# Perceiver on one core: keys and values projected ahead of the first norm, key buffers filled by VectorE, slot zeros written later

## The chip, the core and the metric

The kernel runs on one core of a Trainium2 chip. A core has TensorE (PE in the profile; its weight loads are listed apart as PEld), VectorE (DVE), ScalarE (ACT), GpSimd (POOL) and SyncE (SP), and 16 DMA engines that SP, ACT and POOL can all give transfers to. The metric is the device time of one execution in microseconds (us), the median of several.

## The reference

Two layers of a perceiver: 2 batches of 256 latent rows of 256 numbers, and a context of 4096 rows of 128 numbers for each batch. Everything is float32. Each line adds a block to the residual `x`:

```python
x = x + _L0_xattn_ref(_layernorm(x), ctx_512, Wq, Wkv, Wo)     # 16 heads of 16
x = x + _L0_attn_ref(_layernorm(x), ...)                       # a state-space scan
x = x + _L0_ffn_ref(_layernorm(x), ...)                        # a spectral layer
x = x + _L1_xattn_ref(_layernorm(x), ctx_512, ctx_512, ...)
x = x + _L1_attn_ref(_layernorm(x), ...)
x = x + _L1_ffn_ref(_layernorm(x), ...)                        # 8 experts, 2 per row
```

The change lies in the first of them:

```python
Q = (x @ Wq.T).reshape(B, xN, 16, 16)
KV = (z @ Wkv.T).reshape(B, zN, 2, 16, 16)
K, V = KV[:, :, 0], KV[:, :, 1]
attn = softmax(einsum('bqhd,bkhd->bhqk', Q, K) * SCALE)
O = einsum('bhqk,bkhd->bqhd', attn, V).reshape(B, xN, DIM)
return O @ Wo.T
```

## The kernel before, in words

The first cross attention is the long part. It is cut into 8 groups (2 batches, 4 groups of 4 heads), and each group into 16 steps: 128 steps in all. `attend(n)` writes out one step. Two passes run over the scores. In the first pass (`first`, line 1020 on) a step multiplies the queries `QT[g]` with 512 keys for 4 heads, and VectorE takes the maxima of the products into `MP[G]`. When a group's 16 steps are done, its maxima are lowered into the queries (`greatest`, `lowered`). In the second pass (`second`), 17 steps behind (`LAG`), scores are formed again with keys on the partitions, ScalarE takes the exponentials, and `weigh` multiplies them with the values. So steps 0 to 16 hold the first pass only, and the two passes run side by side from step 17 on.

What a step needs is made a little ahead of it. The dictionary `made` (lines 1149 to 1170) says after which step a piece of work is written down:

- `keys(h2, c)`: one matmul over 512 context columns, two passes of TensorE's instructions, into bank `ps_k`; ScalarE copies it to a piece of `qk`.
- `place(G, c)`: four DMAs of 32 KB that put these keys into the key buffer `KB[G % 3]`, 16 rows in each quarter of the partitions, after row 0 of each quarter, which holds ones. The DMAs of group 1 are issued by ScalarE, all others by SP.
- `values_of(h2, k4)`: a group of values, that is 4 matmuls (8 instructions) over 4 x 128 context rows, into bank `ps_v`; ScalarE copies it into the tile `V`, which has 17 columns for each head: 16 of values and one of ones. The ones and a tail of zeros are written by GpSimd when the tile is new (`k4 == 0`).
- `queries(g)`: one projection (4 instructions) into `ps_q`, which ScalarE scales into `QT[g]`.
- `blank(i, c)`: fills 1024 columns of key buffer `i` with the column `one0` (a one in row 0 of each quarter, zeros elsewhere).

Ahead of step 0 lies the head. The loads of SP are `x`, `wk0`, `wq0`, two quarters of the first context `ctxT[0]`, `wv0`, and the other two quarters. Then come, as written: the norm of `x` (four tiles of 256 columns on VectorE, a square root on ScalarE), eight transposes into `ps_tr` (line 935) with two copies back (lines 937 and 939), `queries(0)`, the copy `wkc` of the key weights without their padding (line 969), the four fills of `KB[0]`, the keys of the first 512 columns for group 0 (line 1176) which go straight into `KB[0]` by ScalarE (line 1177), the work of `made[-1]` (`keys(0, 0)`, `keys(0, 1)`, `place(0, 1)`), and the fills of `KB[1]`.

The PSUM banks are split: `ps1` has four banks, shared by `ps_k`, `ps_v`, `ps_q` and the score tiles of one head (`ps_1`), and `ps2` has two tiles of two banks for the score tiles of two heads (`ps_2`). A step of the first pass takes two banks of `ps1` and one tile of `ps2`.

`route_constants` (line 297) writes small tables for the routing of the last layer, fills half of `O[1]` with zeros and writes these with 15 DMAs of GpSimd's queue to the 15 blocks of `x_slots` in DRAM, which are read at the very end. It is written down after step 50. The loads in `LATE` (steps 20 to 39) begin with a copy of a number out of `MP` into their destination, so that they wait for a step's maxima.

The order on an engine is not the order of the text alone. The program is written with a tile framework that orders each engine's instructions and adds all waits; within its model it lets a later piece go ahead where nothing holds it back. In the part from step 17 on (`in_order`), TensorE, VectorE and ScalarE keep the order of the text for what goes through `te`, `ve` and `se`.

Of the kernel before, what the change touches and what calls it, by code (L numbers as in the profile page):

```python
# [15 lines left out]
P = 128  # L16
B, NQ, D = 2, 256, 256
NT = B * NQ // P
# [32 lines left out]
def perceiver(ctx: ExitStack, tc: tile.TileContext, d: dict, out: bass.AP):  # L51
    nc = tc.nc
# [10 lines left out]
    def bank(name):  # L63
        return ps1.tile([P, 512], F32, tag="bank", name=name)
# [10 lines left out]
    def large(tag, name):  # L75
        return big.tile([P, 4096], F32, tag=tag, name=name)
# [4 lines left out]
    ident = const.tile([P, P], F32, tag="ident", name="ident")  # L81
# [5 lines left out]
    def load(name, shape, src, eng=None):  # L87
        t = const.tile(shape, F32, tag=name, name=name)
        (eng or nc.sync).dma_start(out=t, in_=src)
        return t  # L90

    def load_w(name, eng=None):
        src = d[name]
        k, n = src.shape
        return load(name, [P, k // P, n], src.rearrange("(c p) n -> p c n", p=P), eng)

    x = load("x", [P, NT, D], d["x"].rearrange("(t p) e -> p t e", p=P))
    wk0 = load_w("l0_wk")
    wq0 = load_w("l0_wq")

    one0 = const.tile([P, 1], F32, tag="one0", name="one0")
    nc.gpsimd.memset(one0, 0.0)
# [4 lines left out]
    def load_ctxT(b, c, eng):  # L107
        s = slice(c * NC // 4, (c + 1) * NC // 4)
        eng.dma_start(out=ctxT[b][:, s], in_=d["ctxT"][b, :, s])

    load_ctxT(0, 0, nc.sync)
    load_ctxT(0, 1, nc.sync)
    wv0 = load_w("l0_wv")
    load_ctxT(0, 2, nc.sync)
    load_ctxT(0, 3, nc.sync)
    cols = const.tile([P, 2, d["cols"].shape[1]], F32, tag="cols", name="cols")
# [63 lines left out]
    def rstd_of(mv):  # L180

        n = mv.shape[1]
        r = small.tile([P, n], F32, tag="rstd", name="rstd")
        ve.tensor_scalar_add(r, mv[:, :, 1], EPS)
        ve.reciprocal(r, r)
        yield
        se.activation(r, r, AF.Sqrt)
        yield
        return r
# [18 lines left out]
    def normalised(src, dst, rstd_of=rstd_of):  # L208

        n = src.shape[1]  # L210
        st = small.tile([P, n, 6], F32, tag="bnst", name="bnst")
        mv = small.tile([P, n, 2], F32, tag="bnmv", name="bnmv")
        for t in range(n):
            ve.bn_stats(st[:, t, :], src[:, t, :])
            ve.bn_aggr(mv[:, t, :], st[:, t, :])
            yield
        r = yield from rstd_of(mv)
        for t in range(n):
            ve.tensor_scalar(
                dst[:, t, :], src[:, t, :], mv[:, t, 0:1], r[:, t : t + 1], ALU.subtract, ALU.mult  # L220
            )
            yield
# [20 lines left out]
    def project(ps, w, cs, src):  # L243

        for c in range(2):
            te.matmul(ps, lhsT=w[:, c, cs], rhs=src[:, c, :], start=(c == 0), stop=(c == 1))
# [47 lines left out]
    x_slots = dram.tile([NB * P, D], F32, tag="x_slots", name="x_slots")  # L294
    y_slots = dram.tile([STORED * P, D], F32, tag="y_slots", name="y_slots")

    def route_constants(zeros):
        nc.gpsimd.memset(above, 1.0)
        nc.gpsimd.affine_select(
            out=above, in_=above, pattern=[[1, P]], compare_op=ALU.is_gt, fill=0.0, base=0, channel_multiplier=-1  # L300
        )
        nc.gpsimd.memset(ones, 1.0)
        for t, step, base in ((first_slot, P, 0), (rank, -1, E), (further, 1, 0)):
            nc.gpsimd.iota(
                t, pattern=[[step, t.shape[1]]], base=base, channel_multiplier=0, allow_small_or_imprecise_dtypes=True
            )
        nc.gpsimd.memset(zeros, 0.0)
        for k in range(NB):
            nc.gpsimd.dma_start(out=x_slots[k * P : (k + 1) * P, :], in_=zeros)
# [614 lines left out]
        yield from add_rows(b, o_all, a1_wo, bank)  # L924


    head = large("P", "head")
    xn = head[:, : NT * D].rearrange("p (t e) -> p t e", t=NT)
    xnT = head[:, NT * D : 2 * NT * D].rearrange("p (c n) -> p c n", c=2)
    for _ in normalised(x, xn):  # L930
        pass
    for c in range(2):
        ps = bank("ps_tr")
        for t in range(NT):
            nc.tensor.transpose(ps[:, t * P : (t + 1) * P], xn[:, t, c * P : (c + 1) * P], ident)
        if c:
            nc.scalar.copy(xnT[:, c, :], ps)
        else:
            nc.vector.tensor_copy(xnT[:, c, :], ps)
    O = [acts.tile([P, 2, D], F32, tag=f"O{b}", name=f"O{b}") for b in range(B)]  # L940
    layer0 = ExitStack()
    one = layer0.enter_context(pool("l0x", 1))
# [4 lines left out]
    def queries(g):  # L947
        ps = bank("ps_q")
        project(ps, wq0, slice(g * P, (g + 1) * P), xnT)
        nc.scalar.mul(QT[g], ps, DH**-0.5)  # L950

    queries(0)

# [6 lines left out]
    STEPS = NK // 2  # L962
    LAG = STEPS + 1
    HW = 8 * VW
    VT, MP, AV = {}, {}, {}
# [9 lines left out]
    KB = [large(f"K{i}", f"KB{i}") for i in range(3)]  # L975

    def blank(i, c):

        nc.scalar.copy(KB[i][:, c * 1024 : (c + 1) * 1024], one0.to_broadcast([P, 1024]))

    KC = {}

# [20 lines left out]
    def values_of(h2, k4):  # L1003

        b, half = divmod(h2, 2)
        if k4 == 0:
            vt = big.tile([P, NK * HW + 16], F32, tag=f"V{half}", name="V")
            nc.gpsimd.memset(vt[:, NK * HW :], 0.0)
            nc.gpsimd.memset(vt[:, : NK * HW].rearrange("p (k r) -> p k r", r=VW)[:, :, DH], 1.0)
            VT[h2] = vt  # L1010
        ps = bank("ps_v")
        for c in range(4):
            k = (4 * k4 + c) * P
            te.matmul(
                ps[:, c * P : (c + 1) * P],
                lhsT=ctxT[b][:, k : k + P],
                rhs=wv0[:, 0, half * P : (half + 1) * P],
                start=True,
                stop=True,
            )  # L1020
        se.copy(
            VT[h2][:, 4 * k4 * HW : 4 * (k4 + 1) * HW].rearrange("p (k r) -> p k r", r=VW)[:, :, :DH],
            ps.rearrange("p (k r) -> p k r", r=DH),
        )
# [121 lines left out]
        NM - 14 + i for i, k in enumerate((2, 2, 2, 2, 2, 2, 2, 2, 2, 1, 1, 3)) for _ in range(k)  # L1146
    ]
    chunks = NC // 512
    made = {}
    for h2 in range(B * 2):  # L1150
        for c in range(chunks):
            n0 = max(2 * c - 3, -1) if h2 == 0 else 2 * STEPS * h2 - 19 + 4 * c
            made.setdefault(n0, []).append((keys, h2, c))
            made.setdefault(n0, []).append((place, 2 * h2, c))
            n1 = max(n0, 2 * STEPS * h2 - 12 + 2 * c) if h2 else n0 + 3
            made.setdefault(n1, []).append((place, 2 * h2 + 1, c))
        for k4 in range(NK // 4):
            n0 = 2 * k4 + h2 if h2 < 2 else STEPS * (2 * h2 - 1) + 4 * k4 + 1
            made.setdefault(n0, []).append((values_of, h2, k4))
    for g in range(1, NG):  # L1160
        made.setdefault(4 * g - 1, []).append((queries, g))
    for c in range(4):
        made.setdefault(c, []).append((blank, 2, c))
    for i, f in enumerate(LATE):
        made.setdefault(20 + i, []).append((lambda f=f, i=i: f(MP[(20 + i) // STEPS][:, 0, 0, :1]),))
    made.setdefault(50, []).append((lambda: route_constants(O[1][:, 0, :]),))
    made.setdefault(NM - 10, []).append((spectral_loads,))

    ahead = state_prologue(0, lambda name: bank(name))
    for n in AHEAD:  # L1170
        made.setdefault(n, []).append((next, ahead, None))

    for c in range(4):
        blank(0, c)
    ps = bank("ps_k")
    nc.tensor.matmul(ps, lhsT=wk0[:, 0, :P], rhs=ctxT[0][:, :512], start=True, stop=True)
    nc.scalar.activation(KB[0][:, :512], ps, AF.Identity, bias=one0)
    made[-1].remove((place, 0, 0))
    for f, *at in made[-1]:
        f(*at)  # L1180
    for c in range(4):
        blank(1, c)
    behind = {}

    def attend(n):
# [127 lines left out]
    with pool("ffn", 1) as one:  # L1313
# [38 lines left out]
        ps = bank("ps_n")  # L1352
# [341 lines left out]
```

## Time and profile before

| what | us |
|---|---|
| median of 3 runs (lowest, highest) | 855.04 (854.05, 857.52) |
| the profiled execution, its own time | 854.43 |
| span of its records | 852.7 |
| busy: PE, DVE, ACT, POOL | 806.0, 581.4, 452.5, 46.3 |
| first PE instruction; first score matmul of step 0 | 8.02; 15.87 |
| first score matmul of step 4; of step 16 | 29.23; 62.93 |

The page of the profile gives busy time by engine, 40 slices of the span, and groups of instructions. The timeline lists instructions in order of time; a row has start, length (from the first start to the last end, if several are merged), engine, line, operation, tile written, tile read, how many, and in square brackets how long the engine stood idle before it and for whom. Most helpers are recorded under line 172, so a row is told by its tiles: `ps<-KB,qk` is a score matmul of the first pass, `ps_v` a group of values, `ps_k` keys, `ps_q` queries.

### The profile page before, as it was taken

The numbers are of one execution on the slowest core, as the hardware profiler recorded it, in microseconds if no ns is written. First come the engines' busy times: TensorE is split into PE (matmuls) and PEld (weight loads), VectorE is DVE, ScalarE is ACT, GpSimd is POOL, SyncE is SP. The second block draws the span as 40 slices with busy tenths as digits, with TensorE's granted clock in tenths as the row PEclk, the third lists the DMA queues.
The fourth block names the chain that finished last, engine by engine and source line by source line (L and its number), as shares of the span: only waits on it lengthen the run. The fifth ranks groups of instructions, "written<-read, shape, count | busy, mean of one in ns | idle before, by whom it ended". The sixth has DMA issues, their size and how long they took to land.

```text
span 852.7 us, 21009 instructions
## 1 busy us (share of the span) xinstructions
PE 806.0 (95%) x8626; PEld 576.9 (68%) x8626; DVE 581.4 (68%) x1076; ACT 452.5 (53%) x858; POOL 46.3 (5%) x108
## 2 busy tenths in 40 slices
PE   5998999999999999999988999989799999899996
PEld 3675666666666666666655666865568875799985
DVE  4686888887878787688797766888774588441112
ACT  6434666666667666566664788554534335311110
POOL 5004011000000000000000000000000000030003
PEclk9997999999999999999999999999999999799999
DMA  7215114001101010100000100230205411439602
GB/s 269 55 36 180 26 37 126 17 20 23 24 17 24 11 31 18 23 14 15 2 2 2 50 2 27 75 99 1 99 1 198 165 33 56 144 106 330 207 13 82
DMA packets 35315, 56.67 MB, mean 66 GB/s; under 512 B 5873, under 2 KB 22817, under 8 KB 35217
## 3 DMA queue, kind: packets, MB, share of 16 engines
q1 hardware_dynamic: 27904, 41.44, 16.0%
q0 software_dynamic: 3264, 10.05, 3.5%
q10 hardware_dynamic: 4048, 3.80, 1.6%
q8 instruction: 70, 1.15, 0.5%
q14 instruction: 29, 0.23, 0.1%
HBM read 42.16 MB, written 4.85 MB: 55 GB/s over the span
## 4 chain that ended last, share of the span: by engine, by line
PE 84%; DVE 9%; ACT 4%; issue 2%; DMA 0%; ACTq 0%; DVEq 0%
PE ps L172 29%; PE av L172 17%; PE ps_h L1474 5%; PE ps_y L1490 5%; PE ps_k L172 4%; PE ps_v L172 3%; PE ps_s L172 3%; DVE mp L172 3%; DVE states L172 2%; PE ps_aqk L172 2%; PE ps_in L172 2%; PE ps_pt L172 1%; PE ps_f L172 1%; PE ps_ht L172 1%; PE ps_am L172 1%
## 5 line engine op out<-in xcount | busy, mean ns | idle before, releaser
L172 DVE TENSOR_REDUCE mp<-ps 128x2 f32<-128x1024 f32 (+1 forms) x273 | 303.2, 1154 | 97.8 <-PE ps L172 97.7
L172 ACT ACTIVATE exps<-ps 128x512 f32<-128x512 f32 x512 | 267.1, 603 | 132.3 <-PE ps L172 132.0
L172 PE MATMUL ps<-qk,KB 32*128 32x256 f32 x2048 | 261.8, 398 | 3.4 <-ACT exps L172 1.7
L172 PE MATMUL ps<-KB,qk 32*128 32x256 f32 x2048 | 252.6, 396 | 4.5 <-DVE mp L172 4.5
L172 PEld LDWEIGHTS ps<-KB,qk 32*128 32x128 f32 x2048 | 173.8, 187 | 60.7 <-issue 34.4
L172 PEld LDWEIGHTS ps<-qk,KB 32*128 32x128 f32 x2048 | 188.6, 187 | 18.4 <-ACT exps L172 5.2
L172 PE MATMUL av<-exps,V 128*32 128x256 f32 x2048 | 137.3, 386 | 1.2 <-ACT exps L172 0.8
L172 PEld LDWEIGHTS av<-exps,V 128*32 128x32 f32 x2048 | 53.8, 109 | 63.5 <-ACT exps L172 33.3
L172 DVE TENSOR_TENSOR av<-av 128x256 f32<-128x256 f32 x120 | 49.7, 414 | 5.9 <-PE av L172 5.5
L1481 ACT ACTIVATE room<-ps_h 128x512 f32<-128x512 f32 x24 | 14.2, 598 | 72.3 <-PE ps_h L1474 55.8
L1474 PEld LDWEIGHTS ps_h<-room,w 128*128 128x128 f32 x384 | 44.5, 192 | 0.5
L1474 PE MATMUL ps_h<-room,w 128*128 128x128 f32 x384 | 44.7, 275 | 0.0
L1490 PE MATMUL ps_y<-w,room 128*128 128x256 f32 x192 | 43.3, 379 | 0.0
L172 PEld LDWEIGHTS ps_v<-l_wv,ctxT 128*128 128x128 f32 x256 | 32.6, 191 | 15.2 <-issue 6.2
L172 DVE TENSOR_TENSOR_SCAN states<-decay,ps_in 128x256 f32<-128x256 f32 x64 | 40.0, 670 | 2.5 <-PE ps_in L172 2.5
L1490 PEld LDWEIGHTS ps_y<-w,room 128*128 128x128 f32 x192 | 35.6, 190 | 4.4
L172 PE MATMUL ps_k<-ctxT,wkc 128*128 128x512 f32 x64 | 36.5, 655 | 0.0
L172 PE MATMUL av<-more,nat 128*128 128x256 f32 x128 | 33.4, 384 | 3.0 <-DVE more L172 2.9
L172 PE MATMUL ps_v<-l_wv,ctxT 128*128 128x128 f32 x256 | 35.0, 280 | 1.0 <-ACT V L172 1.0
L172 ACT COPY qk<-ps_k 128x512 f32<-128x512 f32 x32 | 18.7, 588 | 26.8 <-PE ps_k L172 26.5
L172 ACT COPY V<-ps_v 128x512 f32<-128x512 f32 x32 | 18.8, 587 | 20.8 <-PE ps_v L172 15.7
L172 PE MATMUL ps_s<-ctxT,xn 128*128 128x512 f32 x64 | 29.5, 594 | 0.0
(308 smaller groups left out, 862.9 us busy)
## 6 DMA issues: line engine op xcount, KB each, us to landing
w<-in_moe_w SPq DMA_DIRECT2D x24, 1024.0 KB, 7.6
KB<-qk SPq DMA_DIRECT2D x220, 32.0 KB, 2.0
ctxT<-in_ctxT SPq DMA_DIRECT2D x4, 512.0 KB, 8.4
ctxT<-in_ctxT POOLq DMA_DIRECT2D x4, 512.0 KB, 5.7
x_slots<-O POOLq DMA_DIRECT2D x15, 128.0 KB, 6.6
y_slots<-room ACTq DMA_DIRECT2D x10, 128.0 KB, 3.8
room<-x_slots ACTq DMA_DIRECT2D x9, 128.0 KB, 5.0
KB<-qk ACTq DMA_DIRECT2D x32, 32.0 KB, 2.1
```

The source lines that it names most:

```text
L172: i = getattr(self.engine, name)(*args, **kw)
L1474: nc.tensor.matmul(ps[fc // 4][:, (fc % 4) * P : (fc % 4 + 1) * P], lhsT=weights[k][0][:, c, fc * P : (fc + 1) * P], rhs=xT[k][:, c, :], s ...
L1481: nc.scalar.activation(hT[k][:, 4 * i : 4 * i + 4, :].rearrange("p f n -> p (f n)"), ps[i], AF.Silu)
L1490: nc.tensor.matmul(ps[:, :D], lhsT=hT[k][:, fc, :], rhs=weights[k][1][:, fc, :], start=(fc == 0), stop=(fc == NF - 1),)
```

## The change

Five edits:

1. Loads: `wv0` and `wq0` come after the first quarter of the context instead of before it (`wq0`) and after the second (`wv0`).
2. The two first fills of `KB[0]`, the first keys (line 1176) and four groups of values, (0,0), (0,1), (1,0) and (1,1), are written ahead of the norm. Before, these groups came after steps 0, 2, 1 and 3. Norm, transposes and `queries(0)` follow, then the other fills and `made[-1]`.
3. All eight fills of `KB[0]` and `KB[1]` go to VectorE; the four of `KB[2]` stay on ScalarE.
4. The fills of `KB[2]` are written after steps 6 to 9 instead of 0 to 3.
5. The zeros of `x_slots` begin with a copy out of `MP` of step 48's group, so that they and their 15 DMAs wait for that step's maxima.

```diff
     wk0 = load_w("l0_wk")
-    wq0 = load_w("l0_wq")
...
     load_ctxT(0, 0, nc.sync)
+    wv0 = load_w("l0_wv")
+    wq0 = load_w("l0_wq")
     load_ctxT(0, 1, nc.sync)
-    wv0 = load_w("l0_wv")
...
-    def route_constants(zeros):
+    def route_constants(zeros, behind):
...
+        nc.gpsimd.tensor_copy(zeros[:, :1], behind)
         nc.gpsimd.memset(zeros, 0.0)
         for k in range(NB):
             nc.gpsimd.dma_start(out=x_slots[k * P : (k + 1) * P, :], in_=zeros)
...
     def blank(i, c):
-        nc.scalar.copy(KB[i][:, c * 1024 : (c + 1) * 1024], one0.to_broadcast([P, 1024]))
+        o, ones_zeros = KB[i][:, c * 1024 : (c + 1) * 1024], one0.to_broadcast([P, 1024])
+        if i < 2:
+            nc.vector.tensor_copy(o, ones_zeros)
+        else:
+            nc.scalar.copy(o, ones_zeros)
...
+    EARLY = [(0, 0), (0, 1), (1, 0), (1, 1)]
...
         for k4 in range(NK // 4):
+            if (h2, k4) in EARLY:
+                continue
...
     for c in range(4):
-        made.setdefault(c, []).append((blank, 2, c))
+        made.setdefault(6 + c, []).append((blank, 2, c))
...
-    made.setdefault(50, []).append((lambda: route_constants(O[1][:, 0, :]),))
+    made.setdefault(50, []).append((lambda: route_constants(O[1][:, 0, :], MP[50 // STEPS][:, 0, 0, :1]),))
...
-    for c in range(4):
+    made[-1].remove((place, 0, 0))
+    for c in range(2):
         blank(0, c)
+
     ps = bank("ps_k")
     nc.tensor.matmul(ps, lhsT=wk0[:, 0, :P], rhs=ctxT[0][:, :512], start=True, stop=True)
     nc.scalar.activation(KB[0][:, :512], ps, AF.Identity, bias=one0)
-    made[-1].remove((place, 0, 0))
+    for h2, k4 in EARLY:
+        values_of(h2, k4)
+    head = large("P", "head")
...
+    queries(0)
+    for c in range(2, 4):
+        blank(0, c)
+    for c in range(4):
+        blank(1, c)
     for f, *at in made[-1]:
         f(*at)
-    for c in range(4):
-        blank(1, c)
```

The lines of norm, transposes and copies, left out at `head = large(...)`, are the ones that stood before `queries(0)`, unchanged.

More of the change, by code (lines that the diff above doesn't have):

```diff
@@ L924, in self_attention @@
         yield from add_rows(b, o_all, a1_wo, bank)
[L927 to L939, printed above, removed]
     O = [acts.tile([P, 2, D], F32, tag=f"O{b}", name=f"O{b}") for b in range(B)]
@@ L950, in queries @@
         nc.scalar.mul(QT[g], ps, DH**-0.5)
-    queries(0)
     groups = [(b, g) for b in range(B) for g in range(NG)]
@@ L1177, in perceiver @@
     nc.scalar.activation(KB[0][:, :512], ps, AF.Identity, bias=one0)
-    made[-1].remove((place, 0, 0))
+    for h2, k4 in EARLY:
+        values_of(h2, k4)
+    head = large("P", "head")
+    xn = head[:, : NT * D].rearrange("p (t e) -> p t e", t=NT)
+    xnT = head[:, NT * D : 2 * NT * D].rearrange("p (c n) -> p c n", c=2)
+    for _ in normalised(x, xn):
+        pass
+    for c in range(2):
+        ps = bank("ps_tr")
+        for t in range(NT):
+            nc.tensor.transpose(ps[:, t * P : (t + 1) * P], xn[:, t, c * P : (c + 1) * P], ident)
+        if c:
+            nc.scalar.copy(xnT[:, c, :], ps)
+        else:
+            nc.vector.tensor_copy(xnT[:, c, :], ps)
+    queries(0)
[3 more added lines that the diff above has]
+        blank(1, c)
     for f, *at in made[-1]:
         f(*at)
-    for c in range(4):
-        blank(1, c)
     behind = {}
```

## The prediction

> **What bounds the kernel.** I read three views: busy time by engine, the timeline of the first 70 us, and the stretches behind it. The page's first part:
>
> ```profile
> PE 806.0 (95%) x8626; PEld 576.9 (68%) x8626; DVE 581.4 (68%) x1076; ACT 452.5 (53%) x858; POOL 46.3 (5%) x108
> ```
>
> PE is busy 95% of the span, and from step 0 on almost without a break. A microsecond counts if it takes away PE idleness or PE work; no PE work is removed here. So the question is how much later or earlier PE is through with the same instructions. The head, from the timeline:
>
> ```profile
> 4.80 0.75 DVE L172 BATCH_NORM_STATS2 bnst<-x 128x6 f32<-128x256 f32 x2 [4.80 <-DMA x<-in_x]
> 5.30 4.40 POOL L309 DMA_DIRECT2D x_slots<-O  x8 [0.25 <-POOL lowest L843]
> 7.33 1.98 ACT L979 COPY KB<-one 128x1024 f32<-128x1024 f32 x2
> 8.02 2.10 PE L935 MATMUL ps_tr<-ident,head 128*128 128x128 f32 x8 [8.02 <-DVE head L172]
> 9.51 0.69 DVE L939 COPY head<-ps_tr 128x512 f32<-128x512 f32 x1 [0.67 <-PE ps_tr L935]
> 10.26 3.10 PE L172 MATMUL ps_q<-head,l_wq 128*128 128x512 f32 x4
> 14.06 1.88 PE L172 MATMUL ps_k<-ctxT,wkc 128*128 128x512 f32 x4
> 15.87 1.15 PE L172 MATMUL ps<-KB,qk 32*128 32x256 f32 x16
> 17.03 4.75 DVE L172 TENSOR_REDUCE mp<-ps 128x1 f32<-128x512 f32 x6 [6.83 <-PE ps L172]
> 21.23 1.16 PE L172 MATMUL ps_v<-l_wv,ctxT 128*128 128x128 f32 x8 [1.00 <-ACT V L172]
> ```
>
> PE stands until 8.02, when the norm's first tile is there. Step 0 starts at 15.87. There is one stall afterwards: ScalarE, busy with fills, copies a bank of values late, and PE idles 1.0 us before 21.23. Step 4 starts at 29.23. I settle the sum at that point, since from step 4 on both kernels hold the same work.
>
> The weight loads show how fast PE went:
>
> ```profile
> 11.27 0.34 PEld L172 LDWEIGHTS ps_q<-head,l_wq 128*128 128x128 f32 x1 [0.52 <-ACT head L937]
> 12.13 0.34 PEld L172 LDWEIGHTS ps_q<-head,l_wq 128*128 128x128 f32 x1 [0.52 <-issue]
> 12.77 0.19 PEld L1176 LDWEIGHTS ps_k<-ctxT,l_wk 128*128 128x128 f32 x1 [0.30 <-issue]
> 13.20 0.19 PEld L1176 LDWEIGHTS ps_k<-ctxT,l_wk 128*128 128x128 f32 x1 [0.24 <-issue]
> ```
>
> Two loads of the queries' passes (512 columns) lie 0.86 apart, later ones 0.43: PE ran at half speed until about 12.5, 4.5 us after its first instruction, and at full speed from there, though the granted clock of the stretches says 1.00 throughout.
>
> **The order of the loads.** `x` lands at 4.83 (issue 0.83 + 4.0), `wk` at 5.44, `wq` at 6.77, the first quarter of the context at 2.35 + 6.1 = 8.45, `wv` at 11.05. They land in the order of issue. `wq` and a quarter are both 512 KB, so the quarter takes `wq`'s place: 6.77. `wv` (128 KB) follows at about 7.1 (a quarter of the 1.33 that `wq` took), `wq` at about 8.4; the queries need it at 10.3 at the earliest. The 15 DMAs of the slots start at 5.30 and end their issue at 16.78; their going makes no load later, and what they delayed (second quarter on) nobody waited for.
>
> **The work ahead of step 0.** PE can start at 6.85 instead of 8.02, with the first keys. Until step 0 it does, at full speed: first keys 2 x 0.43 = 0.86; four groups of values at 1.09 each (from 21.23 to the next start, 22.32): 4.35; eight transposes, about 1.3 (two took 0.41 at 65.20; bounds 1.1, as eight value instructions, to 2.1, the row above with its waits); queries 1.72; two keys 1.72. Sum 9.95. Added to it: the copy between transposes and queries, of which 0.14 showed as PE idleness; with keys as filling 0, with nothing beside it 0.9; I take 0.3. And the slow start: the values are now the first dense work, done at half speed. If PE speeds up 4.5 us after its first instruction as before, 4.5/2 = 2.25 is lost; if at the same 12.5 on the clock, 2.8; if the wait were 2.3, as counted from the first query matmul (10.26 to 12.5), 1.1. I take 2.25. Step 0 then starts at 6.85 + 9.95 + 0.3 + 2.25 = 19.35, between 18.0 and 20.8.
>
> [...]
>
> So step 0 is 3.5 us later, and the norm's chain is not what it waits for: the transposes queue behind the values on PE (ready at 8 to 11, taken at about 14.3). That is the price of this order.
>
> **Steps 0 to 3.** Before, these took 29.23 - 15.87 = 13.36 and PE was the bound: 4 x 1.08 steps, 4.35 values, keys 2 x 0.97, queries 1.81 and the stall. Without values and stall, PE needs 8.1, but VectorE needs 4.75/2 = 2.37 for the maxima of each step. A step takes a tile of `ps2`, of which there are two, so step 2 waits for the end of step 0's maxima and step 3 for step 1's. With step 0 at t: maxima of step 0 from t+1.16 to t+3.53, of step 1 to t+5.9; step 3 on PE from 5.95 to 7.1, then keys to 8.05, queries to 9.85, step 4 at t+9.85. Of the 13.36 - 9.85 = 3.5 saved nothing is left after the later start: step 4 at 19.35 + 9.85 = 29.2 against 29.23. The gain of the moved values ends at the maxima: VectorE is late next.
>
> **Fills.** ScalarE's fill of 1024 columns takes about 1.0 (1.98 for two). VectorE's nearest row is `wkc<-l_wk`, 0.26 for 256 columns: at least that for a fill, at most 4 x 0.26 = 1.04, which I take, since the work is linear in columns. Two of them lie ahead of the norm: `one0` is ready at 2.6, `x` at 4.83, so they fit in the idle time; put inside the norm they delay it by 2.1, which the values on PE cover. The other six (6.2) lie beside values and transposes: VectorE has nothing else between the norm's end (8.8 to 10.9) and the first maxima at t+1.16 = 20.5 but the copy of 0.69. Cost 0; without this cover, see the third rival. [...]
>
> `KB[2]`'s four fills on ScalarE at steps 6 to 9: copies and DMA issues there come to 4.4 of 5.2 to 6.9 us for two steps, with 2.1 more about 6.4. Between 0 and 0.6; before, the two fills at 23.65 stopped nobody. I take 0, and that ScalarE may well do them earlier, in the emptier head.
>
> **Slot zeros.** The copy waits for step 48's maxima, whose last reduction ends at 177.7 (before, POOL's copies at 124.33 went right after step 32's). Behind it on POOL: the fill of zeros, 15 issues (8.1 at 0.54; 11.5 with the waits seen from 5.30 to 16.78) and the ones of the new `V` tile, at 180.89 before. SP's key DMAs (2.0 each) share the DMA engines then, with steps to spare. `x_slots` is first written again at 750. Cost 0.
>
> **Sum.** 0.0 at step 4, nothing known after it. The profiled execution (span 852.7, own time 854.43) stays at 854.4; it lies 0.6 below the median 855.04, and I put the median at 854.8. About 0.5%, 4.3 us, is what a measurement of this kernel can tell from no change.
>
> **Rivals.** *PE is through earlier* (0.16): it speeds up 2.3 us after its start (-1.1) and takes work of later steps into the 1.8 us where it waits for maxima: 855.0 - 1.1 - 1.8 = 852. For it: the head's order comes from a planner that hoists. Against: the four banks of `ps1` are taken by scores just then.
>
> *The slow stretch after step 16 goes* (0.10). PE has little to do from 64.1 to 67.9, while the maxima are lowered, and the granted clock falls:
>
> ```profile
> 66.00:68.00 2.00, 0.33 (x8) 0.12 (x4) 1.77 (x3) 0.00 (x0) 0.49 (x5) 0.79 0.00 0
> 68.00:70.00 2.00, 2.00 (x20) 1.84 (x24) 0.79 (x1) 0.01 (x1) 2.00 (x11) 0.50 0.00 0
> ...
> 76.00:78.00 2.00, 2.00 (x28) 1.05 (x24) 1.50 (x2) 1.37 (x3) 0.70 (x1) 0.65 1.03 372
> ```
>
> Half clock from about 67.2 to 77.4 costs (77.4 - 67.9)/2 = 4.7. [...] Against: the gap is the same in both.
>
> *Fills in the way* (0.14): if VectorE does all six behind its copy (ending at about 15.7), they end at 21.9, 1.4 after step 0's scores are there, and the maxima bound the next steps; with 0.6 of ScalarE's fills and a start at 20.3: 855 + 1.4 + 0.6 + 1 = 858.
>
> *POOL's queue, slower* (0.08): if the `V` tile's ones come behind all 15 issues and ScalarE's copy of values (182.72) waits for them, it moves to 177.7 + 0.5 + 11.5 + 0.6 = 190.3, and PE with it: 862. It decides from the point where more than about five issues (3.0 us) go ahead of the ones. Against: copy and ones write different columns, and no row shows that wait.
>
> **Numbers.** No change: 0.52, 853.3 to 856.5. Chances of the rivals as given. Range 850.5 to 858.5, leaving out most of the second and the fourth. Faster by over 0.5%: 0.10 (the second); slower: 0.10 (the fourth, and the third's tail); within: 0.80.
>
> **What to look at.** Right: first keys at about 6.85; values at half speed to about 11.3; step 0 at 18 to 21; DVE without idle from step 0 to 3; step 4 within 1 us of 29.2; half clock after step 16; zeros at 178. Wrong: transposes ahead of the values, with step 0 before 17; the first quarter not landed by 7.5; PE busy with later values during steps 0 to 3; a wait of ScalarE near 183.

## The result and the profile after

| what | before | after |
|---|---|---|
| median of 20 runs each | 855.63 | 856.56 |
| ratio of the runs, 95% interval | | 1.0017 [1.0007, 1.0027] |
| the profiled execution, own time; span | 854.43; 852.7 | 856.7; 855.0 |
| step 0; step 2; step 4 | 15.87; 22.32; 29.23 | 19.02; 23.88; 30.86 |

The change made the kernel slower by 0.17%. That is about 1.5 us by the ratio; the medians themselves lie 0.93 apart. The forecast was 0.2 us less than before. Part 1 of the page of after (busy time, share of the span, instructions):

```profile
PE 808.0 (95%) x8626; PEld 579.4 (68%) x8626; DVE 586.3 (69%) x1084; ACT 444.3 (52%) x850; POOL 46.2 (5%) x109
```

PE has the same 8626 instructions and is busy 2.0 us longer with them: some of its work was done more slowly. The head, from the timeline of after (start, length, engine, line, operation, tile written and read, count, and the idle time before with its releaser):

```profile
6.90 2.04 PE L1170 MATMUL ps_k<-ctxT,l_wk 128*128 128x512 f32 x2 [6.90 <-DMA ctxT<-in_ctxT]
8.74 5.27 PE L172 MATMUL ps_v<-l_wv,ctxT 128*128 128x128 f32 x32
10.00 3.70 DVE L967 COPY KB<-one 128x1024 f32<-128x1024 f32 x6
13.85 1.04 PE L1182 MATMUL ps_tr<-ident,head 128*128 128x128 f32 x8
15.28 2.10 PE L172 MATMUL ps_q<-head,l_wq 128*128 128x512 f32 x4 [0.39 <-issue]
17.21 1.88 PE L172 MATMUL ps_k<-ctxT,wkc 128*128 128x512 f32 x4
19.02 2.27 PE L172 MATMUL ps<-KB,qk 32*128 32x256 f32 x32
20.13 42.35 SPq L989 DMA_DIRECT2D KB<-qk  x32
20.19 4.75 DVE L172 TENSOR_REDUCE mp<-ps 128x1 f32<-128x512 f32 x6 [5.01 <-PE ps L172]
21.23 1.13 PE L172 MATMUL ps_k<-ctxT,wkc 128*128 128x512 f32 x2
23.88 3.40 PE L172 MATMUL ps<-KB,qk 32*128 32x256 f32 x32 [1.52 <-DVE mp L172]
25.28 4.75 DVE L172 TENSOR_REDUCE mp<-ps 128x1 f32<-128x512 f32 x6 [0.34 <-PE ps L172]
30.86 1.15 PE L172 MATMUL ps<-KB,qk 32*128 32x256 f32 x16
32.03 4.75 DVE L172 TENSOR_REDUCE mp<-ps 128x1 f32<-128x512 f32 x6 [2.00 <-PE ps L172]
```

The first keys start with the landing of the first quarter at 6.90, and the values behind them take 5.27. Transposes, queries and keys follow, and step 0 starts at 19.02, all close to the forecast. Then come two things that the forecast didn't have. Step 2 starts 4.86 after step 0, with 1.52 of idle time on PE. And steps 2 and 3 together take 3.40 where steps 0 and 1 took 2.27. VectorE then stands too, for 0.34 and 2.00.

The releaser in brackets must be read with care. `DVE mp` is the latest event that the profile sees, but step 0's two maxima, 2.37 in length, were through at 22.6. What was still on its way then were the four DMAs that put the second keys of group 0 into `KB[0]`. ScalarE copies these keys from 19.52 to 20.11 (an issue of a DMA, 18.89 to 19.48, stands before it on that queue), SP issues the four at 20.13, 20.8, 21.7 and 22.4, and they land 2.0 to 2.3 after their issue: the third at about 23.7, the fourth at about 24.4. As written, step 2 begins with the head whose keys the third brings; it starts at 23.88 and has its matmuls close together only from about 24.5 on. Here the cause is inferred from these times; two experiments show it.

The windows of after show why steps 2 and 3 are slow. Columns: stretch, its length, busy time of PE, PEld, DVE, ACT and POOL with counts, granted clock of PE, share of the DMA engines, GB/s:

```profile
22.00:23.00 1.00, 0.35 (x1) 0.00 (x0) 1.00 (x2) 0.00 (x0) 0.00 (x0) 1.00 0.48 103
23.00:24.00 1.00, 0.12 (x1) 0.15 (x2) 1.00 (x3) 0.00 (x1) 0.00 (x0) 1.00 0.49 101
...
25.00:26.00 1.00, 1.00 (x22) 1.00 (x18) 0.72 (x2) 0.00 (x0) 0.00 (x0) 0.81 0.18 39
26.00:27.00 1.00, 1.00 (x11) 0.55 (x6) 1.00 (x2) 0.00 (x0) 0.00 (x0) 0.50 0.35 76
...
29.00:30.00 1.00, 1.00 (x4) 0.47 (x3) 1.00 (x1) 0.59 (x1) 0.00 (x0) 0.99 0.15 33
...
68.00:70.00 2.00, 0.53 (x9) 0.56 (x11) 1.33 (x2) 0.00 (x0) 0.93 (x8) 1.00 0.00 0
70.00:72.00 2.00, 2.00 (x22) 1.95 (x18) 1.23 (x1) 0.94 (x2) 2.00 (x8) 0.50 0.17 33
72.00:74.00 2.00, 2.00 (x8) 0.57 (x4) 1.16 (x1) 1.23 (x3) 2.00 (x4) 0.65 0.92 322
```

PE has little to do from 22.4 to 23.9. At about 25.6 its clock falls to a half and is back at about 29.0, 3.4 later. PE has work in all of that time, so this costs 1.7. Behind step 16 the clock falls again, from 70.0 to 73.4, one third of the stretch that it had in before (67.2 to 77.4). So the profiled execution of after gained there, by a clock that was down for a shorter time. POOL's first copies behind the maxima of step 16 and of step 32 cut the two spans in three: up to the first, after took 1.6 longer (69.07 against 67.51), between them 2.8 less (54.0 against 56.8), and behind the second 3.5 longer. One profiled execution can't tell this change's worth.

The zeros of the slots are as forecast, and nobody waits for them (POOL's rows of after):

```profile
176.52 0.19 POOL L307 COPY O<-mp 128x1 f32<-128x1 f32 x1 [47.28 <-DVE mp L172]
177.38 8.01 POOL L310 DMA_DIRECT2D x_slots<-O  x15 [0.30 <-POOL O L308]
```

### The profile page after: what moved, and what is told of

Read it like the earlier page. It is cut to its first block, busy times and chain, and to the rows that moved or that the text cites. A ratio compares the mean times of both kernels' runs of the same rounds, so it can differ in the third digit from the quotient of the medians.

```text
span 855.0 us, 21003 instructions
## 1 busy us (share of the span) xinstructions
PE 808.0 (95%) x8626; PEld 579.4 (68%) x8626; DVE 586.3 (69%) x1084; ACT 444.3 (52%) x850; POOL 46.2 (5%) x109
## 3 DMA queue, kind: packets, MB, share of 16 engines
HBM read 42.16 MB, written 4.85 MB: 55 GB/s over the span
## 4 chain that ended last, share of the span: by engine, by line
PE 85%; DVE 9%; ACT 3%; issue 2%; DMA 1%; SPq 0%; DVEq 0%; ACTq 0%
PE ps L172 29%; PE av L172 17%; PE ps_h L1485 5%; PE ps_y L1501 5%; PE ps_k L172 4%; PE ps_v L172 3%; DVE mp L172 3%; PE ps_s L172 3%; DVE states L172 2%; PE ps_aqk L172 2%; PE ps_in L172 2%; PE ps_pt L172 1%; PE ps_f L172 1%; PE ps_ht L172 1%; PE ps_am L172 1%
## 5 line engine op out<-in xcount | busy, mean ns | idle before, releaser
L172 PE MATMUL ps<-qk,KB 32*128 32x256 f32 x2048 | 258.9, 395 | 3.4 <-ACT exps L172 1.7
L172 PEld LDWEIGHTS ps<-qk,KB 32*128 32x128 f32 x2048 | 186.6, 185 | 18.0 <-ACT exps L172 5.6
L1492 ACT ACTIVATE room<-ps_h 128x512 f32<-128x512 f32 x24 | 14.2, 597 | 75.7 <-PE ps_h L1485 67.2
L1509 DVE COPY room<-ps_y 128x256 f32<-128x256 f32 x10 | 4.2, 425 | 37.2 <-PE ps_y L1501 37.2
```

The costliest lines, as they stand in the source:

```text
L172: i = getattr(self.engine, name)(*args, **kw)
L1492: nc.scalar.activation(hT[k][:, 4 * i : 4 * i + 4, :].rearrange("p f n -> p (f n)"), ps[i], AF.Silu)
L1509: nc.vector.tensor_copy(Y[k], ps[:, :D])
```

## The experiments

*Theory:* step 2 waits for the second keys' DMAs; the idle time on PE makes the clock fall to a half for 3.4 us; this is what the change costs. *Rivals:* the zeros or the fills cost it; or the values ahead of the norm, by themselves; or the difference lies behind step 16, where the clock falls in both kernels for a time that differs between executions.

The steps' starts are from one profile each. The last three columns are against runs of before on the same chip. "Half clock" is worked out for each run from its mean granted clock: (1 - clock) x span is the time lost to the half clock, since a stretch T at half clock lowers the mean by T/2 of the span and costs T/2 of work where PE is the bound. The slow start of the head isn't in it, since the granted clock reads 1.00 there (from 8 to 12 in after, where the values ran at half speed). "Rest" is the run's time less that. Both are differences of means with 95% bounds; the ratio is that of the comparison.

| kernel | step 0 | step 2 | step 4 | half clock, us | rest, us | ratio |
|---|---|---|---|---|---|---|
| a0_again | 17.90 | 22.74 | 29.76 | +2.6 (1.3) | -1.4 (0.7) | 1.0014 [1.0000, 1.0028] |
| e1_zeros | 15.34 | 21.79 | 28.70 | 0.0 (0.9) | -0.5 (1.0) | 1.0000 [0.9986, 1.0014] |
| e3_keys_ahead | 19.63 | 22.62 | 29.43 | -1.3 (1.1) | -0.7 (0.7) | 0.9977 [0.9964, 0.9990] |
| e4_busy | 18.06 | 23.03 | 28.25 | -1.9 (1.0) | -0.9 (0.7) | 0.9968 [0.9956, 0.9979] |
| e4_again | 19.17 | 24.14 | 29.35 | -1.0 (1.7) | -0.7 (0.7) | 0.9976 [0.9957, 0.9995] |
| e5_two_groups | 16.36 | 21.21 | 29.22 | -1.2 (1.0) | +0.3 (0.7) | 0.9992 [0.9976, 1.0008] |
| e6_no_groups | 15.06 | 20.48 | 27.42 | +0.1 (1.5) | -1.4 (0.9) | 0.9978 [0.9960, 0.9996] |
| e6_again | 17.64 | 23.06 | 30.33 | -0.2 (1.5) | -1.5 (1.0) | 0.9979 [0.9961, 0.9998] |
| e10_keys_none | 15.28 | 20.46 | 27.67 | +0.8 (1.1) | -1.8 (0.7) | 0.9985 [0.9970, 0.9999] |
| e7_fills_act | 18.93 | 25.10 | 32.08 | +2.7 (2.9) | +3.4 (1.2) | 1.0071 [1.0046, 1.0096] |
| f1_gap_e6 | 17.47 | 22.89 | 30.47 | -3.1 (1.6) | -1.1 (1.6) | 0.9942 [0.9920, 0.9965] |
| f2_gap_before | 16.51 | 22.96 | 29.87 | -4.7 (0.9) | +0.6 (1.1) | 0.9949 [0.9930, 0.9968] |
| f2_again | 15.71 | 22.16 | 29.07 | -4.7 (0.7) | +1.0 (0.9) | 0.9960 [0.9944, 0.9976] |
| g1_gap_after | 19.05 | 23.90 | 30.92 | -3.0 (1.1) | -0.1 (0.8) | 0.9965 [0.9950, 0.9979] |
| g2_gap_busy | 19.54 | 24.52 | 29.72 | -3.4 (1.0) | +0.1 (0.7) | 0.9962 [0.9947, 0.9977] |
| g3_gap_keys | 18.71 | 21.70 | 28.51 | -2.4 (1.1) | -0.8 (0.8) | 0.9958 [0.9943, 0.9972] |

**a0_again**: after once more, no edit.

> The changed kernel once more, unchanged. Theory A (head): step 2 waits for the four DMAs that bring the second 512 columns of keys into the key buffer, some 1.2 us longer than for the maxima, PE stands idle meanwhile, and its clock falls to half for one window of 3.4 us. Then step 2 starts 4.8 to 4.9 us after step 0 again (the wait is fixed), and step 4 starts 11.8 us after step 0 if the clock falls, 10.3 to 10.6 if it doesn't; ratio to before 1.0005 to 1.003. Theory B (slot zeros at step 48 cost the time): the same ratio, whatever the head does. Theory C (chance of where later half-clock stretches fall): ratio 0.999 to 1.001.

The total of +1.2 us is the difference of two opposite terms: 2.6 more is lost to the half clock, and 1.4 is saved. The half clock stood in steps 2 and 3 here too (23.4 to 26.8).

**e1_zeros**: before, with the hold of the zeros alone.

```diff
-    def route_constants(zeros):
+    def route_constants(zeros, behind):
...
+        nc.gpsimd.tensor_copy(zeros[:, :1], behind)
         nc.gpsimd.memset(zeros, 0.0)
```

> The kernel before with the fifth edit alone: the slot zeros wait for step 48's maxima. Theory A: nothing on the path, ratio 0.999 to 1.001, step 4 at 29.2 as before. Theory B: the whole loss is here, ratio 1.001 to 1.003.

No difference: the zeros are no part of the cause.

**e3_keys_ahead**: after, with `keys(0, 0)`, `keys(0, 1)` and `place(0, 1)` written ahead of the values.

```diff
+    for f, *at in made.pop(-1):
+        f(*at)
     for h2, k4 in EARLY:
         values_of(h2, k4)
...
-    for f, *at in made[-1]:
-        f(*at)
```

> The changed kernel with the keys of the first 1024 columns and their DMAs written ahead of the four groups of values, behind the first keys. Theory A: the DMAs land long before step 2, so step 2 starts about 3.6 us after step 0 and step 4 about 9.9 after it; step 0 itself 0.3 to 0.8 later than the 19.0 of the changed kernel, since nothing covers the scaling of the queries; step 4 at 29.2 to 29.8 (30.9 in the changed kernel), ratio to before 1.000 (0.999 to 1.001). Theories B and C: ratio as the changed kernel's, 1.0007 to 1.0027, with the head's times not mattering.

The DMAs leave SP from 12.86 on. From the timeline of e3_keys_ahead:

```profile
19.63 2.01 PE L172 MATMUL ps<-KB,qk 32*128 32x256 f32 x32 [0.69 <-ACT qk L938]
22.62 0.69 PE L172 MATMUL ps<-KB,qk 32*128 32x256 f32 x2
23.86 1.56 PE L172 MATMUL ps<-KB,qk 32*128 32x256 f32 x18 [0.55 <-DVE mp L172]
25.59 1.13 PE L172 MATMUL ps<-KB,qk 32*128 32x256 f32 x12 [0.17 <-DVE mp L172]
29.43 1.15 PE L172 MATMUL ps<-KB,qk 32*128 32x256 f32 x16
```

Step 2 now starts 2.99 after step 0 and then waits for the maxima, in pieces of 0.55 and 0.17. The clock stays at 1.00, and step 4 comes 9.80 after step 0: the sequence that the forecast worked out for after (9.85) is the one of this kernel. It takes 3.1 us (1.1) less than a0_again on the same chip, more than the head explains, and its ratio lies below the one expected.

**e4_busy**: after, with the key matmul that stands between steps 1 and 2 done three times into the same bank; the products are the same. It leaves the way of the DMAs as it is and fills the idle time with work.

```diff
+        for _ in range(2 if (h2, c) == (0, 2) else 0):
+            te.matmul(
+                ps, lhsT=wkc[:, half * P : (half + 1) * P], rhs=ctxT[b][:, c * 512 : (c + 1) * 512],
+                start=True, stop=True,
+            )
```

> The changed kernel with the key matmul after step 1 done three times into the same bank: 2 us more work for PE in the gap ahead of step 2, nothing else. Theory A: the gap is filled (step 2 starts within 0.4 us of where it did), the clock stays full, and step 4 starts earlier than the changed kernel's 30.9 though PE does more, at 29.2 to 29.9; ratio 0.9995 to 1.001. If the fall of the clock costs nothing, step 4 is 0.2 to 2 us later than 30.9 and the ratio 1.002 to 1.004.

```profile
18.06 2.27 PE L172 MATMUL ps<-KB,qk 32*128 32x256 f32 x32
20.26 2.84 PE L172 MATMUL ps_k<-ctxT,wkc 128*128 128x512 f32 x6
23.03 2.51 PE L172 MATMUL ps<-KB,qk 32*128 32x256 f32 x32
28.25 1.23 PE L172 MATMUL ps<-KB,qk 32*128 32x256 f32 x16
```

Step 2 still comes 4.97 after step 0, about where it came in after (4.86). But PE has work until then, so the wait itself can't be seen here; the clock stays at 1.00, and steps 2 and 3 take 2.51 instead of 3.40. Step 4 comes 10.19 after step 0 instead of 11.84, though PE does 1.7 us more. This separates the two halves of the theory, in the head: of the 2.0 by which step 4 missed its forecast, about 1.7 is the clock and the rest the wait. In time the kernel gains more than that: 4.0 (1.0) against a0_again. One half-clock stretch of 3.4 (1.7 us) is located; the rest isn't.

**e6_no_groups** and **e5_two_groups**: after, with no values and with two groups of values ahead of the norm.

```diff
-    EARLY = [(0, 0), (0, 1), (1, 0), (1, 1)]
+    EARLY = []
```

> The changed kernel with no group of values moved: all sixteen stand after steps 0 to 15 as before, the first keys, the loads, the fills and the zeros as in the change. Theory A (values ahead of the norm only push step 0 back, and steps 0 to 3 without them are bound by the maxima and a DMA wait): step 0 at 13.5 to 15.0, step 4 some 12.4 us later (4 steps 4.3, values 3 of 4 beside 3.3 and the fourth 1.1, keys 1.9, queries 1.8) at 26.0 to 27.5, clock full through the steps; ratio to before 0.996 to 0.9985. If the moved values were what saves time and something else loses it: step 4 at 31 or later, ratio 1.002 or more.

> The changed kernel with two groups of values, (0,0) and (1,0), ahead of the norm instead of four. Theory A: step 0 2.2 us earlier than the changed kernel's (18 to 19), at 15.8 to 16.9; step 2 again 4.8 to 4.9 after step 0 (the DMA wait); the two groups left after steps 2 and 3 lie partly beside the maxima; step 4 at about 12.0 after step 0, 27.8 to 28.9, or one more if the clock falls; ratio 0.998 to 1.001, between the changed kernel and the one with no group moved. Otherwise (the number of groups doesn't matter): as the changed kernel, 1.001 to 1.003.

Without values step 0 is there at 15.06, step 4 at 27.42, and the other edits save 1.4 (0.9) at unchanged half clock. In total, none, two and four groups give -1.3 (1.3), -0.9 (1.0) and +1.2 (0.9) against before, the last on another chip. None and four have the same rest; what four groups cost against none is the half clock, +2.6 against +0.1. Why two groups have a higher rest than both stays open.

The head of e5_two_groups is a caution for the theory:

```profile
21.21 1.77 PE L172 MATMUL ps<-KB,qk 32*128 32x256 f32 x16 [1.52 <-DVE mp L172]
```

Step 2 comes 4.85 after step 0 behind the same idle time of 1.52, and yet the clock stays at 1.00. So the clock falls behind this wait in some executions and not in others. It did in all three profiles with four groups and nothing in the gap (after, a0_again, g1_gap_after), and not in this one; the last section comes back to it. Step 4, at 29.22, is later than expected all the same, since two groups of values lie in these steps. So the other edits are worth having, and the values moved ahead gain nothing over none.

**e7_fills_act**: after, with all fills on ScalarE.

```diff
-        if i < 2:
-            nc.vector.tensor_copy(o, ones_zeros)
-        else:
-            nc.scalar.copy(o, ones_zeros)
+        nc.scalar.copy(o, ones_zeros)
```

> The changed kernel with all fills on ScalarE (third edit undone). Theory A: fills on VectorE are hidden and worth having: here ScalarE's 8 us of them lie between the copies of values, PE waits for banks, step 0 at 20 to 23 instead of 18 to 19, step 4 at 31 to 34; ratio 1.002 to 1.006. Rival (fills in VectorE's way cost the time): step 0 to 3 earlier by 0.5 to 1.5, ratio 0.999 to 1.0005.

```profile
21.19 1.63 PE L172 MATMUL ps<-KB,qk 32*128 32x256 f32 x16 [1.11 <-ACT qk L172]
18.67 1.98 ACT L966 COPY KB<-one 128x1024 f32<-128x1024 f32 x2
20.55 1.07 ACT L172 COPY qk<-ps_k 128x512 f32<-128x512 f32 x2
...
25.10 4.27 PE L172 MATMUL ps<-KB,qk 32*128 32x256 f32 x32 [1.23 <-DMA KB<-qk]
```

The fills stand before the copies of the keys on ScalarE, the DMAs leave later, and step 2 comes 6.17 after step 0. Here the trace names the DMA itself as the releaser. Step 1 waits too, 1.11 for a copy of keys, and behind step 4 PE waits 1.17 for another. Step 0 is not pushed back (20 to 23 had been expected). The fills on VectorE are the good part of the change, and these waits say that they matter by way of ScalarE's queue.

**e10_keys_none**: e6_no_groups with the keys ahead of the norm, as in e3_keys_ahead.

> The changed kernel with no group of values moved and with the keys of the first 1024 columns and their DMAs right behind the first keys, ahead of the norm. Theory A: keys fill PE's time until the norm is there; step 0 at 14.8 to 16.0, since nothing covers the scaling of the queries, and step 4 12.4 later at 27.2 to 28.4: between the kernel with no group moved and before; ratio 0.9965 to 0.9995.

It is much like e6_no_groups in steps and time: with the values gone, the DMAs are in time anyway: PE's rows of both show no idle time from step 0 to step 4.

**f1_gap_e6** and **f2_gap_before**: e6_no_groups and before, each with three unread matmuls added in the gap behind step 16 (one before the lowering of the maxima, two behind its transposes).

```diff
+            if n == STEPS:
+                ps = bank("ps_work")
+                te.matmul(ps, lhsT=wkc[:, :P], rhs=VT[1][:, 28 * HW : 28 * HW + 512], start=True, stop=True)
             if n and i == 0 and n <= NM:
                 lowered(G - 1)
+                if n == STEPS:
+                    ps = bank("ps_work")
+                    for _ in range(2):
+                        te.matmul(
+                            ps, lhsT=negm[:, 0, :, :].rearrange("p j r -> p (j r)"),
+                            rhs=VT[1][:, 28 * HW : 28 * HW + 512], start=True, stop=True,
+                        )
```

In the two texts that follow, "the gate" is the author's supposition that the fall of the clock behind step 16 follows PE's idle time ahead of it. The runs show the idle time and the clock, not what ties the two together.

> The kernel with no group of values moved, and in the gap after step 16, where the maxima are lowered, three more matmuls whose results nobody reads (one ahead of the two transposes, two behind). Theory A with the gate: the time of all these kernels moves by the number of half-clock windows after step 16. From the first copy behind step 16's maxima to the first behind step 32's the profiles so far show 52.4 (no half clock), 54.0 (one window) and 56.8 (three); with PE busy in the gap it is 52.3 to 52.8, half clock absent there; ratio to before 0.993 to 0.9965. If half clock after step 16 is not due to the idle gap: 54 or 56.8 as before and the ratio of the kernel without this filling, 0.9975 to 0.9985, or worse by the 2.6 us of added work.

> The kernel before with the same three matmuls in the gap after step 16, nothing else. Theory A with the gate: interval from step 16's to step 32's copies 52.3 to 52.8 instead of 56.8; the mean loss there over the ten profiles so far is 2.3, so ratio 0.9965 to 0.998. Otherwise: ratio 1.000 to 1.003.

The windows of f2_gap_before, the same stretches that the forecast showed of before:

```profile
66.00:68.00 2.00, 1.84 (x6) 0.68 (x5) 2.00 (x4) 0.00 (x0) 0.00 (x0) 1.00 0.00 0
68.00:70.00 2.00, 2.00 (x31) 1.69 (x32) 0.90 (x3) 0.38 (x1) 1.86 (x13) 1.00 0.00 0
...
76.00:78.00 2.00, 2.00 (x37) 1.06 (x33) 2.00 (x3) 1.73 (x4) 0.72 (x1) 1.00 1.06 386
```

The clock stays at 1.00 where it had been 0.50. The distance between two copies of POOL, those that wait for the maxima of step 16 and of step 32, shows the price: 52.3 with the fill in all six profiles that have it, and 52.4, 54.0, 55.1 or 56.8 to 56.9 without it, by how long the clock was down. 2.6 us of unread work (six passes of 0.43) saves 4.7 (0.9) of half clock. Both kernels are faster than before and after.

**e4_again**, **e6_again** and **f2_again**: the same kernels on another chip.

> The changed kernel with the key matmul after step 1 done three times, once more, beside the kernel with no group moved. Theory A: step 4 starts 10.2 us after step 0, at 28.2 to 29.3, clock full there; that is worth 0.5 to 1.0 us against before, so ratio 0.998 to 1.0, not below the kernel with no group moved. If its 0.9968 repeats, some 2 us come from behind step 4, which the head does not explain.

> The changed kernel with no group of values moved, once more. Theory A: step 0 at 14.5 to 15.5, step 4 at 26.9 to 27.9, ratio 0.9965 to 0.999.

> The kernel before with three unread matmuls in the gap after step 16, once more, as the measure for the next three. Interval from step 16's to step 32's copies 52.3; ratio to before 0.9935 to 0.9965.

The ratios hold. The head of e6 does not: step 0 stood at 15.06 and now at 17.64. The queries' rows of e6_no_groups, then of e6_again:

```profile
11.43 1.98 PE L172 MATMUL ps_q<-head,l_wq 128*128 128x512 f32 x4 [0.58 <-DVE head L1186]
```

```profile
11.69 3.78 PE L172 MATMUL ps_q<-head,l_wq 128*128 128x512 f32 x4 [0.57 <-DVE head L1186]
```

The same four instructions, at the same place, at full and at half speed: when PE speeds up in a thin head differs by execution.

**g1_gap_after**, **g2_gap_busy** and **g3_gap_keys**: after, e4_busy and e3_keys_ahead, each with the three matmuls of f2.

> The changed kernel with the same three matmuls after step 16. Interval 52.3. If the head alone makes the difference between the two kernels (step 4 at 30.9 and 29.8 against 29.2, 28.7 and 29.9): 1.0 us (0.4 to 1.8) above the kernel before with the filling, ratio to before 0.995 to 0.998. If it was the windows after step 16: no difference.

> The changed kernel with the key matmul after step 1 done three times and the three matmuls after step 16. Interval 52.3, clock full in steps 0 to 16. From step 4 at 28.3 and 29.4: 1.5 us (0.8 to 2.2) below the changed kernel with the filling alone, 0.5 (0 to 1.2) below the kernel before with it; ratio to before 0.9925 to 0.9955. If the 2 us more that it gained lie in the head, 2.5 below the kernel before with the filling.

> The changed kernel with the keys of the first 1024 columns and their DMAs ahead of the values, and the three matmuls after step 16. Interval 52.3. From step 4 at 29.4: within 0.7 us of the kernel before with the filling, 0.9 (0.2 to 1.6) below the changed kernel with it; ratio to before 0.9935 to 0.9965.

With the gap behind step 16 out of the way, the rival that places the cost there can be weighed. Between g1_gap_after and f2_again the change is +0.6 us (0.7): 1.65 (1.0) more half clock, as much as one stretch of 3.4 us costs, and -1.0 (1.0) of the rest. So both terms of a0_again are there without the gap. But that the 1.65 is the stretch in the head isn't shown: g2's profile has no such stretch, and its runs still have 1.3 (0.9) more half clock than those of f2_again. And g2 and g3, which take the fall or the wait away, gain only 0.1 (0.8) and 0.2 (0.8) on g1 where up to 1.7 was to be had; e4's surplus over the located 1.7 is gone too. The bounds leave room for some 1.0 of the 1.7. That the surplus of e4 and e3 came from the gap behind step 16 is argued from its going with the fill, not shown.

The profiles hold a point ahead of all this: POOL's first copy behind step 16's maxima. In before, then in after:

```profile
67.51 0.54 POOL L134 COPY ctxT<-mp 128x1 f32<-128x1 f32 x4 [50.73 <-DVE mp L172]
```

```profile
69.07 0.55 POOL L134 COPY ctxT<-mp 128x1 f32<-128x1 f32 x4 [64.27 <-DVE mp L172]
```

In the four profiles with the head of before it stands at 67.0 to 68.1 (mean 67.5), in the three of after's head at 68.0 to 69.1 (68.7), and in the five with the idle time filled or the keys ahead (e3, g3, e4, e4_again, g2) at 66.5 to 68.2 (67.4). So up to step 16 the change costs 1.2 in these profiles, and taking the idle time away gives it back. They are few, and their ranges touch; where the rest of a run's half clock falls, behind step 16 and from 430 on, differs between executions of one kernel (granted clock from 440 to 640 and from 640 to 720: 0.99 and 0.98 in after, 0.98 and 1.00 in a0_again).

## Why the prediction was wrong

- *First keys at 6.85, values at half speed, step 0 at 19.35*: right in its course. They were at 6.90 and 19.02 (step 0 at 17.90 and 19.05 in a0 and g1). But two of its terms were off and made up for each other, which is luck. The value instructions of after, in the windows 8.6 to 11.7 and 12.2 to 13.9:

```profile
L172 PE MATMUL ps_v<-l_wv,ctxT x14: 418/418/418, 8.7 to 11.5; 128*128 128x128 f32 x14
L172 PE MATMUL ps_v<-l_wv,ctxT x17: 275/275/287, 11.9 to 13.7; 128*128 128x128 f32 x17
```

  They took 418 ns each, and from about 12.0 on 275; they started 0.21 and then 0.11 apart. At 0.11 the 32 of them would take 3.5, not 4.35: the row of 1.09 for a group came from steps with other work between. And half speed lasted 5.1 us after the first instruction, and cost some 2.5 (an estimate): 0.9 in the first keys (2.04 instead of the 1.13 of the same work at 21.23) and 1.6 in the values. In a0_again the values took 4.29 instead of 5.27: by an estimate from this they were at full speed from about 9.8 on and some 1.5 was lost. Step 0 came 1.1 earlier, just outside the stated 18.0 to 20.8. So the loss belongs to the execution.
- *Step 2 waits for the end of step 0's maxima, at t + 3.6*: **this step failed**. The forecast asked which PSUM tile step 2 needs and not which keys. `place(0, 1)` stands in no term of its sum; its way, a copy on ScalarE, four issues on SP and the landing, was thereby put at nothing. The runs put t + 4.84 to t + 4.98 in its place, in all six profiles of kernels with the four groups, VectorE's fills and the keys behind them.
- *Step 4 at t + 9.85*: the second half of the failure. It was t + 11.84, 11.86 and 11.87 (after, a0, g1): the wait, and 1.7 for the stretch at half clock that followed it in these three. With the keys ahead it was t + 9.80. The sum was thus right for a kernel that does not wait.
- *VectorE without idle in steps 0 to 3*: wrong with it, 0.34 and 2.00.
- *Cost 0 for the fills*: right. Six in a row took 3.70 and one alone 0.69, against my bound of 1.04 each: four times the columns of the 0.26 row took 2.7 times as long. They ended at 13.70, ahead of the transposes' copy, so the third rival had no case. `KB[2]`'s fills were done early by ScalarE (7.38 to 15.72).
- *Cost 0 for the zeros*: right, and no wait near 183; the fourth rival fell.
- *The slow stretch after step 16 is the same in both*: wrong as put. Its length belongs to the execution and not to the kernel, from none to three times 3.4 us in unfilled kernels (POOL's copies lay 56.8 apart in e6_no_groups and 52.4 in e6_again, one kernel). The second rival was a real thing, but one that the change doesn't govern.
- *Sum 0.0 at step 4*: by the means of the runs, 1.0 to 1.4 saved and 1.7 to 2.6 lost to the clock, in the two pairs (g1_gap_after and f2_again, a0_again and before): +0.6 and +1.2. The head is the place of up to 1.7 of what was lost. Where the saving lies is only partly located: without its slow stretch, after's step 4 would stand at 28.8 (mean of three profiles), and that of before is at 29.2 (mean of the four profiles with its head).

## What to carry to other kernels

When a step is moved, follow each operand of the first instruction behind it to its DMA: the tile it writes is only one of its waits. Price a wait of PE twice, once for its length and once for the clock that it may bring down (here a fall of 3.4 us, worth 1.7, followed in three profiles of four with the same idle time of 1.5), and see whether work that is at hand can fill it; here 2.6 us of unread matmuls saved 4.7 of half clock (f2_gap_before). Where the time lost depends on how an execution falls on such stretches, compare many runs, and take the clock's share out of each before comparing.

## What the runs showed of the hardware

- In the profiles of after and before the clock fell and rose at times that lie whole multiples of 3.41 us apart: in after 25.6, 29.0, 70.0 (13 times 3.41 behind 25.6) and 73.4; in before it sped up at 12.5, fell at 67.2 (16 times) and rose at 77.4 (three more). So each has a grid of 3.41, and the two grids lie differently from the start of the span: before's 67.2 is 12.2 times 3.41 behind after's 25.6.
- An idle time of 1.51 or 1.52 ahead of step 2 was followed by a fall of the clock, 0.7 to 1.8 us after its end, in after, a0_again and g1_gap_after, and by none in e5_two_groups; one of 1.00 in before (ahead of 21.23) by none (clock 1.00 from 20 to 26). In e5 the idle time has another place on the grid. Two stretches of the grid of after, then two of e5 (its grid is an estimate, counted back in steps of 3.41 from the fall at 68.64 behind step 16):

```profile
22.20:25.61 3.41, 1.89 (x23) 1.42 (x26) 3.06 (x5) 0.59 (x1) 0.00 (x0) 1.00 0.35 76
25.61:29.02 3.41, 3.41 (x19) 1.78 (x13) 3.41 (x6) 0.00 (x0) 0.00 (x0) 0.50 0.33 67
```

```profile
17.44:20.85 3.41, 2.25 (x22) 1.08 (x17) 3.32 (x5) 0.01 (x1) 0.00 (x0) 1.00 0.39 84
20.85:24.26 3.41, 3.05 (x28) 2.29 (x32) 3.07 (x5) 0.59 (x1) 0.00 (x0) 1.00 0.30 66
```

  In after the whole idle time lies in one stretch, and PE is busy for 1.89 of it (1.90 and 1.89 in a0 and g1); in e5 the border at 20.85 cuts it in two. That this decides is argued from four profiles, not shown. Busy time alone doesn't decide it: in before the clock stayed at 1.00 behind a stretch with 1.72 (439.21 to 442.62), among other instructions.
- More work made a kernel faster: 1.7 us more in e4_busy (4.0 (1.0) less than a0_again) and 2.6 us more in f2_gap_before (ratio to before 0.9949).
- One float32 fill of 128x1024 from a column took 0.69 on VectorE (six in a row 3.70) and 1.03 to 1.07 on ScalarE, both in after.
